# The end of layer 1 by halves of the nodes, with fewer wide operations, beside layer 2's products

## The chip, the cores and the metric

The kernel runs on one core of a Trainium2 chip. The metric is the device time of one execution in microseconds (us); smaller is better.

## The reference

Four graph layers run one after the other on 4096 nodes with 64 features, over one dense 4096 x 4096 adjacency matrix of zeros and ones. Each layer normalises x, clips it at zero to h, and adds the layer's result to x:

```
h = maximum(layernorm(x), 0)
x = x + layer(h, adj)
```

Layer 0 is graph attention with eight heads. Layer 1 works in a ball: for every pair of nodes it computes a sigmoid weight and a logarithmic map, sums them to one vector per node (`support_t`), and finishes node by node:

```
def mobius_add(x, y, c):
    x2, y2, xy = sum(x*x), sum(y*y), sum(x*y)
    num = (1 + 2*c*xy + c*y2) * x + (1 - c*x2) * y
    return num / clip(1 + 2*c*xy + c*c*x2*y2, MIN_NORM)
def expmap(p, u, c):
    u_norm = norm(u)
    return mobius_add(p, tanh(0.5*sqrt(c)*lambda_x(p, c)*u_norm) * u / (sqrt(c)*u_norm), c)
out = proj(expmap(x, support_t, c), c)      # proj: scale down where the norm is too large
```

Layer 2 averages the neighbours (`adj @ X + X` over the degree), multiplies by a matrix, and normalises each row. Layer 3 sums each row's last hundred neighbours with weights that fall by a half.

## The kernel before

Node number b*128 + p stands on partition p, in column b, so `x` and `h` are tiles of 128 partitions x 32 columns x 64 features. An operation over all of it has 128x2048 elements; `halves` names the two halves of 16 columns, 128x1024 each. A number for each node (a norm, a dot product) is a tile of 128x32, or 128x16 for a half.

**Order of the work.** A planner orders each engine's instructions by its own costs, keeping data dependences; a block under `in_order()` keeps its own order on VectorE, ScalarE and TensorE, though the planner may put other instructions between those of the block. Pools of on-chip memory are opened and closed as a stack: a tile in a new pool waits for the tiles that stood there before.

**Layer 1, pairs** (`pairs_fast`). Blocks of pairs are worked through on TensorE, ScalarE and VectorE; the sums collect in `VT` (128 x 4096), from the accumulators `acci` and `accj` (L2260, L2291, L2292, L2318). The products `pvt` (L2347, 32 in 8 groups) fold VT and turn it to nodes, and VectorE puts each group, scaled by `pabs`, into `VQ` (L2351): 64 features and one number per node. In the trace each of these fp32 products appears as two records. VT's memory belongs to the pairs' pool, and the pvt products have banks of their own.

**Layer 1, end** (`finish`). All nodes at once, on VectorE: `dot` multiplies two wide tiles and reduces (L2036, L2038), `norm_of` takes a root on ScalarE (L2043, L2044), and wide products with one number per node (`over`) follow (L2357 to L2397). Each intermediate vector is formed in full width, and its norm and dot products are then taken from it. The last step adds to x (L2397).

**Layer norm** (`layernorm_relu`, L966 to L976), for each half: mean, subtract, square on VectorE (`ln_sq`, L970), reduce (`ln_var`, L972), root on ScalarE (L973), reciprocal, multiply (L975), maximum (L976). It is called before layers 1, 2 and 3, and with another pool before layer 0.

**Layer 2** (`layers_fast`). `HH` holds h in two halves of precision; it is made in four groups of 8 columns (hs and HH, L2439 to L2442). For each half of the targets (hf) and each of 8 mask tiles `m` of 1 MB (L2448; three buffers), TensorE runs 16 products `nacc` (L2453) and 16 `dc`, which count neighbours (L2465). A tile covers four of the 32 columns, so the first four tiles of a pass read half 0 of the nodes and the last four half 1. A tail of small steps per half follows (L2473 to L2530).

**The edge test** (`count_odd`, L949 and L950). The adjacency has to be 0 or 1 throughout; 64 strips `raw` of 1 MB each are loaded and tested on VectorE, with two buffers, wherever the text places them: 12 in layer 2, 36 in layer 3. In layer 2 the text places one after the nacc products of each mask tile but every fourth:

```
if q % 4 != 3:
    count_odd(work, next(todo))
```

Layer 3 starts with loads of its weights (w3f), products psup and the steps SS and lo (L2595 to L2602).

Of the kernel before, what the change touches and what calls it, by code (L numbers as in the profile page):

```python
# [24 lines left out]
P = 128  # L25
# [805 lines left out]
def kernel(  # L831
# [124 lines left out]
    def small(name, width=NB):  # L956
        return spool.tile([P, width], F32, name=name, tag=name)

    def layernorm_relu(pool=None, tag="wide"):
        with ExitStack() as ln:  # L960
            wide = pool or ln.enter_context(tc.tile_pool(name="ln", bufs=1))
            for bs in halves:
                nb = bs.stop - bs.start
                hb = h[:, bs]
                mean = small("ln_mean", nb)
                nc.vector.tensor_reduce(mean, x[:, bs], AX.X, ALU.add)  # L966
                nc.vector.tensor_scalar(mean, mean, 1.0 / D, None, ALU.mult)
                nc.vector.tensor_tensor(hb, x[:, bs], over(mean, D), ALU.subtract)
                sq = wide.tile([P, nb, D], F32, name="ln_sq", tag=tag)
                nc.vector.tensor_tensor(sq, hb, hb, ALU.mult)  # L970
                var = small("ln_var", nb)
                nc.vector.tensor_reduce(var, sq, AX.X, ALU.add)  # L972
                nc.scalar.activation(var, var, AF.Sqrt, bias=eps_t, scale=1.0 / D)  # L973
                nc.vector.reciprocal(var, var)
                nc.vector.tensor_tensor(hb, hb, over(var, D), ALU.mult)  # L975
                nc.vector.tensor_scalar(hb, hb, 0.0, None, ALU.max)  # L976
# [1028 lines left out]
    def scalar_tile(name):  # L2005
        return lp.tile([P, 1], F32, name=name)
# [7 lines left out]
    c2, m2c, cneg, lnr, bz, be, maxn, hrow = (  # L2014
        scalar_tile(n) for n in ("c2", "m2c", "cneg", "lnr", "bz", "be", "maxn", "hrow")
    )
    nc.vector.tensor_tensor(c2, cc, cc, ALU.mult)
    nc.vector.tensor_scalar(m2c, cc, -2.0, None, ALU.mult)
    nc.vector.tensor_scalar(cneg, cc, -1.0, None, ALU.mult)
# [86 lines left out]
    def pairs_fast(es, VQ):  # L2106
# [12 lines left out]
        pabs = fp.tile([P, NB], F32, name="pabs")  # L2119
# [49 lines left out]


        VT = fp.tile([P, N], F32, name="VT")
        work = es.enter_context(tc.tile_pool(name="pfwork", bufs=2))
        with ExitStack() as ss:
# [162 lines left out]
        nc.vector.tensor_scalar(pabs, pabs, sqc, 2.0, ALU.mult, ALU.mult)  # L2336
        fold_v = work.tile([P, D1], F32, name="fold_v", bufs=1)
        nc.vector.tensor_copy(fold_v[:, 0:D], ident[:, 0:D])
        nc.vector.tensor_tensor(
            fold_v[:, D:], ident[:, D + 31 : D + 32], ident[:, P - 1 :], ALU.add  # L2340
        )
        with tc.tile_pool(name="ps_vt", bufs=2, space=PSUM) as ps:
            for g in range(NG):
                pt = ps.tile([P, GB, D1], F32, name="pvt", tag="misc")
                for b in range(GB):
                    c = (g * GB + b) * P
                    nc.tensor.matmul(  # L2347
                        pt[:, b, :], lhsT=VT[:, c : c + P], rhs=fold_v, start=True, stop=True
                    )
                bs = slice(g * GB, (g + 1) * GB)  # L2350
                nc.vector.tensor_tensor(VQ[:, bs, :], pt, over(pabs[:, bs], D1), ALU.mult)  # L2351

    def finish(VQ, wide, lp):

        V = VQ[:, :, 0:D]
        qq = dot(wide, lp, h, V, "xv")
        nc.vector.scalar_tensor_tensor(qq, qq, m2c, VQ[:, :, D], ALU.mult, ALU.add)  # L2357
        u = V
        nc.vector.tensor_tensor(u, u, over(pc, D), ALU.mult)
        t = wide.tile([P, NB, D], F32, name="hq", tag="wide")  # L2360
        nc.vector.tensor_tensor(t, h, over(qq, D), ALU.mult)
        nc.vector.tensor_tensor(u, u, t, ALU.subtract)
        rowf = small("rowf")
        nc.vector.tensor_scalar(rowf, pm, hrow, None, ALU.mult)
        nc.vector.tensor_tensor(u, u, over(rowf, D), ALU.mult)
        un = norm_of(lp, dot(wide, lp, u, u, "uu"), "un")
        nc.vector.tensor_scalar(un, un, sqc, None, ALU.mult)
        arg = small("arg")
        nc.vector.reciprocal(arg, pm)
        nc.vector.tensor_tensor(arg, arg, un, ALU.mult)  # L2370
        nc.scalar.activation(arg, arg, AF.Tanh)
        nc.vector.reciprocal(un, un)
        nc.vector.tensor_tensor(arg, arg, un, ALU.mult)
        nc.vector.tensor_tensor(u, u, over(arg, D), ALU.mult)

        y2 = dot(wide, lp, u, u, "y2")
        xy = dot(wide, lp, h, u, "xy")
        nc.vector.tensor_scalar(xy, xy, m2c, -1.0, ALU.mult, ALU.mult)
        nc.vector.tensor_scalar(xy, xy, 1.0, None, ALU.add)
        num = small("mnum")  # L2380
        nc.vector.scalar_tensor_tensor(num, y2, cc, xy, ALU.mult, ALU.add)
        den = small("mden")
        nc.vector.tensor_tensor(den, a, y2, ALU.mult)
        nc.vector.scalar_tensor_tensor(den, den, c2, xy, ALU.mult, ALU.add)
        nc.vector.tensor_scalar(den, den, MIN_NORM, None, ALU.max)
        nc.vector.reciprocal(den, den)
        nc.vector.tensor_tensor(u, u, over(pc, D), ALU.mult)
        t = wide.tile([P, NB, D], F32, name="hn", tag="wide")
        nc.vector.tensor_tensor(t, h, over(num, D), ALU.mult)
        nc.vector.tensor_tensor(u, u, t, ALU.add)  # L2390
        nc.vector.tensor_tensor(u, u, over(den, D), ALU.mult)

        nn = norm_of(lp, dot(wide, lp, u, u, "pp"), "nn")
        nc.vector.reciprocal(nn, nn)
        nc.vector.tensor_scalar(nn, nn, maxn, 1.0, ALU.mult, ALU.min)
        nc.vector.tensor_tensor(u, u, over(nn, D), ALU.mult)
        nc.vector.tensor_tensor(x, x, u, ALU.add)  # L2397

# [5 lines left out]
    def layers_fast(es):  # L2404
# [16 lines left out]
        layernorm_relu()  # L2421
        with ExitStack() as l2:
# [12 lines left out]
            OG = 8  # L2435
            for b0 in range(0, NB, OG):
                bs = slice(b0, b0 + OG)
                hs = work.tile([P, OG, D], F32, name="hs", tag="hs")
                nc.vector.tensor_scalar(hs, h[:, bs], VALH, None, ALU.mult)  # L2439
                nc.scalar.copy(HH[:, bs, 0, :], hs)  # L2440
                nc.vector.tensor_tensor(hs, hs, HH[:, bs, 0, :], ALU.subtract)
                nc.scalar.activation(HH[:, bs, 1, :], hs, AF.Copy, scale=LO)  # L2442
            for hf in range(2):
                accs = [ps_acc.tile([P, G], F32, name="nacc", tag="nacc") for _ in range(NS)]
                dc = ps_acc.tile([P, G], F32, name="dc", tag="nacc")
                for q in range(NQ):
                    m = work.tile([P, JT, HW], U8, name="m2", tag="m2", bufs=3)
                    nc.sync.dma_start(m, mask_d[q][hf])  # L2448
                    m8 = m.bitcast(F8)
                    for t in range(JT):  # L2450
                        j = q * JT + t
                        for k in range(NS):
                            nc.tensor.matmul(  # L2453
                                accs[k],
                                lhsT=HH[:, j].rearrange("p s d -> p (s d)"),
                                rhs=m8[:, t, k * G : (k + 1) * G],
                                start=(j == 0),
                                stop=(j == NB - 1),
                            )
                    if q % 4 != 3:  # L2460
                        count_odd(work, next(todo))
                    for t in range(JT):
                        j = q * JT + t
                        for k in range(NS):
                            nc.tensor.matmul(  # L2465
                                dc[k * O : (k + 1) * O, :],
                                lhsT=sel[:, j * O : (j + 1) * O],
                                rhs=m8[:, t, k * G : (k + 1) * G],
                                start=(j == 0),
                                stop=(j == NB - 1),  # L2470
                            )
# [202 lines left out]
    def after_pairs(pairs):  # L2674
        with ExitStack() as es:
            vp = es.enter_context(tc.tile_pool(name="vq", bufs=1))
            VQ = vp.tile([P, NB, D1], F32, name="VQ")
            with ExitStack() as pe:
                pairs(pe, VQ)
            wide = es.enter_context(tc.tile_pool(name="finwide", bufs=2))  # L2680
            fl = es.enter_context(tc.tile_pool(name="fin", bufs=1))
            finish(VQ, wide, fl)

    with tc.If(general == 0):
        after_pairs(pairs_fast)
        with ExitStack() as es:
            layers_fast(es)
# [61 lines left out]
```

## Time and profile before

| what | us |
|---|---|
| median of 3 runs | 2256.92 (2254.91 to 2257.21) |
| the profiled execution, its own time | 2256.87 |
| its span | 2254.9 |
| TensorE (PE) busy | 1920.0 (85%) |
| VectorE (DVE) busy | 1780.3 (79%) |
| ScalarE (ACT) busy | 1588.5 (70%) |
| last acci product of the pairs ends | 1810.9 |
| first nacc product of layer 2 starts | 1889.25 |
| layer 2's nacc and dc products end | about 1974.7 |

The profile is one execution. PE is TensorE's products, PEld its weight loads, POOL GpSimd, SP the engine that issues most transfers. A row of the timeline has start, length, engine, line and operation, tiles and shapes; "x2" means two merged. In the chain that ended last each row has start, length and what the end of the program waited for then. In the waits, "A <- B: 74.6, 1, 74.6" says that A's engine sat idle before A until B ended, in total, how often, and the longest.

### The profile page before, as it was taken

The page shows a single profiled execution, that of the slowest core. Times are in us where ns is not written, and L with a number is a line of the kernel's source. Part 1 is how long each engine was busy: PE and PEld are TensorE (multiplying, and loading weights), DVE is VectorE, ACT ScalarE, POOL GpSimd, SP SyncE. Part 2 cuts the span into 40 slices and gives each one's busy share as a digit, 9 for nine tenths or more (in the row PEclk, how much of TensorE's full clock was granted, in tenths as well). Part 3 has the DMA queues.
Part 4 walks back from the last instruction along what each step waited for, and adds up shares of the span by engine and source line. Part 5 has one row for each costly group of instructions (what it writes and reads, how often), then busy time and mean ns, then how long its engine had stood idle before and what let it go on. Part 6 is the DMA issues. An engine that isn't in the chain of part 4 may idle for free.

```text
span 2254.9 us, 43716 instructions
## 1 busy us (share of the span) xinstructions
PE 1920.0 (85%) x19276; PEld 870.7 (39%) x19276; DVE 1780.3 (79%) x2092; ACT 1588.5 (70%) x1338; POOL 86.2 (4%) x124
## 2 busy tenths in 40 slices
PE   4989989999999999769982789999999914959998
PEld 3444444444444444424441233333333401434332
DVE  6689889987898899797657899898898887463551
ACT  4678888996898799467853788888888800124765
POOL 1000101100000000001101000000000000000000
PEclk8999999999999999779996799999999966956998
DMA  9945554352111110477630001110011007624883
GB/s 112 182 100 94 91 90 114 128 192 86 44 63 67 45 52 2 145 255 252 193 109 24 18 23 33 38 33 24 28 33 38 15 0 266 257 92 176 314 313 98
DMA packets 117007, 239.00 MB, mean 106 GB/s; under 512 B 11059, under 2 KB 84003, under 8 KB 102051
## 3 DMA queue, kind: packets, MB, share of 16 engines
q1 hardware_dynamic: 101990, 192.92, 24.9%
q0 software_dynamic: 14816, 43.18, 10.8%
q8 instruction: 153, 2.51, 0.5%
q14 instruction: 48, 0.39, 0.1%
HBM read 245.34 MB, written 49.46 MB: 131 GB/s over the span
## 4 chain that ended last, share of the span: by engine, by line
PE 34%; DVE 15%; DMA 6%; ACT 4%; issue 4%; POOL 0%; SPq 0%; DVEq 0%; POOLq 0%; ACTq 0%
PE accj L2260 6%; DMA raw<-in_adj_dram 5%; PE acco L1948 5%; PE pu L2227 3%; PE nacc L2453 3%; PE pl L2196 2%; PE pf L2298 2%; PE pl L2199 2%; DVE at L2249 2%; DVE raw L950 2%; PE accC L1521 2%; DVE at L2254 1%; PE ddo L1961 1%; PE accB L1521 1%; PE tr L982 1%
## 5 line engine op out<-in xcount | busy, mean ns | idle before, releaser
L1185 ACT ACTIVATE st<-srow,nt 128x2048 int8<-128x2048 f32 x352 | 682.8, 1994 | 77.4 <-DVE B L1191 76.5
L1191 DVE TENSOR_TENSOR B<-st,mres 128x1024 int32<-128x1024 int32 x256 | 311.8, 1220 | 66.4 <-PE accC L1521 41.5
L1521 PE MATMUL accB<-B,ybh 128*32 128x512 fp8e4 x3072 | 338.1, 383 | 15.6 <-DVE B L1191 15.6
L1521 PE MATMUL accD<-B,ybh 128*32 128x512 fp8e4 x2048 | 300.5, 386 | 23.8 <-DVE h L1637 23.8
L1521 PEld LDWEIGHTS <-ybh 128*32 128x32 bf16 (+1 forms) x6656 | 196.6, 98 | 238.7 <-issue 76.4
L1521 PE MATMUL accC<-B,ycn 128*32 128x512 fp8e4 x2272 | 266.6, 379 | 1.2 <-issue 1.2
L1521 PE MATMUL accC<-mres,ych 128*32 128x512 fp8e4 x2272 | 266.6, 379 | 0.0
L1521 PE MATMUL accL<-B,ybh 128*32 128x512 fp8e4 x1536 | 219.6, 389 | 4.6 <-DVE h L1641 4.5
L950 DVE SCALAR_TENSOR_TENSOR raw<-raw 128x2048 f32<-128x2048 f32 x64 | 146.3, 2288 | 92.0 <-DMA raw<-in_adj_dram 92.0
L2260 PE MATMUL accj<-sg,VQ 128*64 128x512 f32 (+1 forms) x512 | 198.3, 615 | 18.6 <-DVE VT L2318 7.1
L1521 PEld LDWEIGHTS <-ych 128*32 128x32 f16 x4096 | 168.2, 98 | 114.0 <-issue 8.2
L1179 DVE TENSOR_SCALAR st<-srow,nt 128x2048 uint8<-128x2048 f32 x160 | 205.5, 1285 | 2.5
L2260 PE MATMUL acci<-sg,VQ 128*64 128x512 f32 (+1 forms) x512 | 197.7, 615 | 0.0
L2183 ACT ACTIVATE sg<-pl,rb 128x512 f32<-128x512 f32 x256 | 163.1, 684 | 47.3 <-PE pl L2199 43.3
L2644 ACT ACTIVATE w3b<-pv 128x1024 int16<-128x1024 f32 x128 | 131.1, 1024 | 54.6 <-PE pv L2635 54.3
L1185 ACT ACTIVATE st<-srowo,nto 128x1024 int8<-128x1024 f32 x128 | 137.3, 1137 | 42.0 <-DVE B L1191 41.8
L2227 PE MATMUL pu<-XAf,LDf 66*128 66x512 f32 x288 | 149.1, 621 | 7.2 <-DVE at L2234 5.9
L1521 PE MATMUL accC<-C,ych 128*32 128x512 fp8e4 x1824 | 145.9, 388 | 0.8 <-DVE C L1199 0.8
L1199 DVE TENSOR_TENSOR C<-B,mres 128x1024 int32<-128x1024 int32 x114 | 139.6, 1225 | 3.6
L1521 PEld LDWEIGHTS <-ycn 128*32 128x32 f16 x2272 | 107.3, 97 | 63.5 <-issue 2.4
L2453 PE MATMUL nacc<-m,HH 128*128 128x512 fp8e4 x256 | 62.0, 391 | 74.6 <-ACT HH L2442 74.6
L2234 DVE TENSOR_SCALAR at<-pu 128x512 f32<-128x512 f32 x144 | 95.2, 684 | 22.7 <-PE pu L2227 21.9
(491 smaller groups left out, 3144.2 us busy)
## 6 DMA issues: line engine op xcount, KB each, us to landing
raw<-in_adj_dram SPq DMA_DIRECT2D x64, 1024.0 KB, 7.3
mo<-edges SPq DMA_DIRECT2D x32, 512.0 KB, 4.8
noedge<-nmo POOLq DMA_DIRECT2D x32, 512.0 KB, 5.0
nm<-noedge SPq DMA_DIRECT2D x64, 256.0 KB, 3.0
m<-edges SPq DMA_DIRECT2D x16, 1024.0 KB, 6.2
m<-edges SPq DMA_DIRECT2D x32, 512.0 KB, 5.9
srow<-srow_d SPq DMA_DIRECT2D x15, 1024.0 KB, 6.5
mres<-in_adj_dram POOLq DMA_DIRECT2D x8, 1024.0 KB, 35.9
```

Source lines behind the costliest of these rows:

```text
L950: nc.vector.scalar_tensor_tensor(raw, raw, 0.0, raw, ALU.is_gt, ALU.not_equal, accum_out=bad[:, c : c + 1])
L1179: nc.vector.tensor_scalar(st[:, i, :].bitcast(U8), srow, negs[:, i : i + 1], EDGE, ALU.is_gt, ALU.mult)
L1185: nc.scalar.activation(st[:, i, :], srow, AF.Sign, bias=negs[:, i : i + 1], scale=-1.0)
L1191: nc.vector.tensor_tensor(B.bitcast(I32), st.bitcast(I32), edges.bitcast(I32), ALU.bitwise_and)
L1199: nc.vector.tensor_tensor(C.bitcast(I32), B.bitcast(I32), edges.bitcast(I32), ALU.bitwise_xor)
L1521: ins = nc.tensor.matmul(acc[k * O : (k + 1) * O, :], lhsT=values, rhs=moving(k), start=start, stop=stop,)
L1948: sums = nc.tensor.matmul(acc[k], lhsT=Y[:, i].rearrange("p s d -> p (s d)"), rhs=E[:, i, k * G : (k + 1) * G], start=j0 + i == 0, stop=ac ...
L2183: tc.keep_in_program_order(nc.scalar.activation(*args, **kw))
L2227: nc.tensor.matmul(pu, lhsT=LD[:, j * P : (j + 1) * P], rhs=XA[:, grp(gi)], start=True, stop=True,)
L2260: nc.tensor.matmul(acc[r : r + n, :], lhsT=XQ[:, src, cols], rhs=w, start=start, stop=stop)
L2453: nc.tensor.matmul(accs[k], lhsT=HH[:, j].rearrange("p s d -> p (s d)"), rhs=m8[:, t, k * G : (k + 1) * G], start=(j == 0), stop=(j == NB ...
L2644: nc.scalar.activation(w, pv, AF.Relu)
```

## The change

1. `finish` becomes `finish_steps`, a generator for one half of the nodes. The norms and dot products of the intermediate vectors are worked out from numbers by node: `xu` (h with the sum), `uu` (its square norm), `a` (h with itself). The vector itself is formed once at the end, as one factor (`arg`) times V plus another (`num`) times h. The one square that remains is on ScalarE (`vv`).
2. The pvt products and VQ's evictions move into `finish_steps`. VT, `fold_v` and `pabs` move to the pool that also holds VQ and stays open through layers 2 and 3; `fold_v` is set before the pairs.
3. Layer norm is a generator too (`norm_steps`). Its square goes to ScalarE (not before layer 0), and multiply and maximum become one VectorE instruction. `finish_steps` ends with it.
4. HH is made by halves, in the same generator (`nodes`), without the first wide multiply.
5. `side_by_side` runs half 0's steps; at each point where half 0 waits for another engine it takes two steps of half 1, ten at most. The rest of half 1 follows. All of it stands under `in_order()`.
6. In layer 2's text the edge tests stand in tiles 4 to 7 of the first pass and in all of the second, 12 as before.

```diff
+    def norm_steps(bs, wide, tag, act=True):
...
+        nc.vector.tensor_reduce(mean, x[:, bs], AX.X, ALU.add)
+        yield False
+        nc.vector.tensor_scalar(mean, mean, 1.0 / D, None, ALU.mult)
+        nc.vector.tensor_tensor(hb, x[:, bs], over(mean, D), ALU.subtract)
+        yield False
+        sq = wide.tile([P, nb, D], F32, name="ln_sq", tag=tag)
+        if act:
+            nc.scalar.activation(sq, hb, AF.Square)
+        else:
+            nc.vector.tensor_tensor(sq, hb, hb, ALU.mult)
+        yield act
+        var = small("ln_var", nb)
+        nc.vector.tensor_reduce(var, sq, AX.X, ALU.add)
+        nc.scalar.activation(var, var, AF.Sqrt, bias=eps_t, scale=1.0 / D)
+        yield True
+        nc.vector.reciprocal(var, var)
+        nc.vector.scalar_tensor_tensor(hb, hb, 0.0, over(var, D), ALU.max, ALU.mult)
+        yield False
...
+    def side_by_side(first, second, fill, most):
+        for wait in first:
+            for _ in range(min(fill, most) if wait else 0):
+                next(second)
+                most -= 1
+        for _ in second:
+            pass
...
+    nc.vector.tensor_scalar(p2c, cc, 2.0, None, ALU.mult)
...
-    def finish(VQ, wide, lp):
...
+    def finish_steps(hf, VQ, VT, fold_v, pabs, wide, ps):
...
+        for g in range(hf * NG // 2, (hf + 1) * NG // 2):
+            pt = ps.tile([P, GB, D1], F32, name="pvt", tag="misc")
...
+            nc.vector.tensor_tensor(VQ[:, gs, :], pt, over(pabs[:, gs], D1), ALU.mult)
+            yield g % 2 == 0
+        t = fat("xv")
+        nc.vector.tensor_tensor(t, hb, V, ALU.mult)
+        yield False
+        xu = scal("xu")
+        nc.vector.tensor_reduce(xu, t, AX.X, ALU.add)
+        yield False
...
+        nc.vector.tensor_tensor(t, hb, over(g, D), ALU.mult)
+        yield False
+        nc.vector.tensor_tensor(V, V, t, ALU.subtract)
+        t = fat("vv")
+        nc.scalar.activation(t, V, AF.Square)
+        yield True
...
+        nc.vector.tensor_reduce(uu, t, AX.X, ALU.add)
...
+        nc.scalar.activation(un, un, AF.Sqrt)
+        yield True
...
+        nc.scalar.activation(arg, arg, AF.Tanh)
+        yield True
...
+        nc.scalar.activation(pp, pp, AF.Sqrt)
...
+        yield True
...
+        nc.vector.tensor_tensor(V, V, over(arg, D), ALU.mult)
+        yield False
+        t = fat("xn")
+        nc.vector.tensor_tensor(t, hb, over(num, D), ALU.mult)
+        yield False
+        nc.vector.tensor_tensor(V, V, t, ALU.add)
+        yield False
+        nc.vector.tensor_tensor(x[:, bs], x[:, bs], V, ALU.add)
+        yield False
+        yield from norm_steps(bs, wide, "fat")
...
-        layernorm_relu()
...
+            def nodes(hf):
+                yield from finish_steps(hf, *sums, wide, ps)
+                bs = halves[hf]
+                hs = wide.tile([P, HB, D], F32, name="hs", tag="fat")
+                nc.scalar.activation(HH[:, bs, 0, :], h[:, bs], AF.Copy, scale=VALH)
+                yield True
+                nc.vector.scalar_tensor_tensor(
+                    hs, h[:, bs], VALH, HH[:, bs, 0, :], ALU.mult, ALU.subtract
+                )
+                nc.scalar.activation(HH[:, bs, 1, :], hs, AF.Copy, scale=LO)
+
+            with in_order():
+                side_by_side(nodes(0), nodes(1), 2, 10)
...
-                    if q % 4 != 3:
+                    if hf or q >= NQ // 2:
                         count_odd(work, next(todo))
```

## The prediction

> **What bounds the kernel now.** I read the busy time by stage first: the stretches are the end of layer 1's pairs, the end of layer 1, and layer 2's two passes. Columns are length, then busy time of PE, PEld, DVE, ACT, POOL, granted clock, DMA share, GB/s.
>
> ```profile
> 1754.00:1811.00 57.00, 54.63 (x303) 23.62 (x296) 44.91 (x42) 42.20 (x42) 0.00 (x0) 1.00 0.05 14
> 1811.00:1889.20 78.20, 2.08 (x16) 1.80 (x16) 73.39 (x67) 7.00 (x11) 3.82 (x6) 0.53 0.21 81
> 1889.20:1928.10 38.90, 38.85 (x257) 15.23 (x258) 19.02 (x21) 3.98 (x7) 0.00 (x0) 0.93 0.89 326
> 1928.10:1974.70 46.60, 46.51 (x344) 23.98 (x344) 24.37 (x48) 7.57 (x18) 2.23 (x5) 1.00 0.59 225
> ```
>
> From 1811.0 to 1889.2 VectorE alone works (73.4 of 78.2 us). Before it and after it TensorE is full. The waits of TensorE say the same, in one entry:
>
> ```profile
> PE nacc L2453 <- ACT HH L2442: 74.6, 1, 74.6
> ```
>
> The timeline gives the prices: a half-size operation, a strip of the edge test (raw), a dependent pair of small ones.
>
> ```profile
> 1881.74 1.21 DVE L975 TENSOR_TENSOR h<-h,ln_var 128x1024 f32<-128x1024 f32 x1
> 1888.46 2.28 DVE L950 SCALAR_TENSOR_TENSOR raw<-raw 128x2048 f32<-128x2048 f32 x1
> 1890.67 0.68 DVE L2441 TENSOR_TENSOR hs<-hs,HH 128x512 f32<-128x512 f32 x1
> 1850.93 0.23 DVE L2378 TENSOR_SCALAR xy<-xy,m2c 128x32 f32<-128x32 f32 x1
> 1851.20 0.18 DVE L2379 TENSOR_SCALAR xy<-xy 128x32 f32<-128x32 f32 x1
> ```
>
> A strip holds VectorE 2.21 us (1888.46 to 1890.67). Half-size operations start 1.14 us apart where independent, 1.25 where one needs the other; I take 1.20. Small ones are 0.08 to 0.27 apart; I take 0.18. The last thing to read is where pvt, the products that fold VT, lie now (chain that ended last), and how long a strip's transfer takes (tile raw, 1886 to 1896, then 2060 to 2215):
>
> ```profile
> 1781.72 1.73 PE pvt L2347 x16
> 1787.35 1.29 PE pvt L2347 x12
> DMA to landing us min/median/max: 5.1/5.1/5.1
> ...
> DMA to landing us min/median/max: 5.6/7.3/8.1
> ```
>
> So most pvt products stand in the full TensorE stage today, and a strip lands in 5.1 us when it has the queues nearly to itself, 7.3 when it shares them with layer 3's masks.
>
> [...]here layer 2's first 16 products take 6.11 us against 3.56 later, and that stays.[...] a load is 1.28 us here, and the changed order holds six small activations with five loads, behind which VectorE has other work.
>
> **Part 1, the end of layer 1.** Let T0 be the end of the last pairs product (acci, 1810.93 now). Today it takes 4.2 us to the first wide operation, 54.3 for `finish` (21 full-width operations), 16.6 for the norm and 3.2 for HH: 78.3 us to the first nacc product. In the built program I counted what stands on VectorE between T0 and the first half's HH:
> - three moves into VT, 0.69+0.71+0.72 = 2.1 us;
> - all eight VQ evictions, since pvt now waits for the last VT sum and for the banks of the pairs: TensorE makes a group in 0.55 us (8 in 1.11 us for two), so 8×0.55+0.5 = 4.9;
> - 19 half-size operations, 14 of half 0 and 5 of half 1, ×1.20 = 22.8;
> - 53 small ones ×0.18 = 9.5;
> - **all 12 strips of layer 2**. In the text of the kernel they stand behind the products, but the built order pulls them in between the steps of half 0. 12×2.22 = 26.6;
> - what ScalarE leaves open: the norm's root 0.45, the HH copy 1.2, its low part 1.3 (128x1024 on ScalarE takes 1.14 in layer 0): 2.95. The squares, tanh and the other roots have a strip or other steps beside them.
>
> The sum is 68.9. Today one strip lies there, and a second starts as the stage ends. The strips' transfers start at T0, three masks first: 5 MB at the 420 GB/s of 1870 to 1882 is 12.5 us, and VectorE reaches the first strip at about T0+14.5. After that a strip is asked for when the one two before it is done, 5.4 to 7.5 us before its turn. At 5.1 us nothing waits; at 7.3 a pair of strips takes 9.5 us instead of about 8.2, up to 6.5 us in all. I take 1.5. First nacc at T0+70.4: **−7.9 us**, between −9.5 and −2.
>
> **Part 2, half 1 beside the products.** Behind half 0 VectorE has 9 half-size operations (11), 27 small (4.9) and open ScalarE steps (4.2): HH of half 1 at about T0+89.2. TensorE needs it after four mask tiles: 70.4 + 7.1 (cold) + 3×4.53 = T0+91.1. Hidden, by under 2 us; late by up to 3 in the range. The fourth mask waits for the first tile's release and has 9 us to land: enough. Layer 2's passes stay 38.9 + 46.6, since TensorE is full in both now; taking the strips out of them gains nothing.
>
> **Part 3, T0 itself.** The pvt pieces before T0 add up to 4.3 us on the chain (the two above, and 0.37, 0.17, 0.39, 0.17, 0.17). TensorE is 96% busy there, so their going should show; VectorE and ScalarE (79% and 74%) can take some back. −1.5 to −4.3, I take **−3**. Three small reductions (qsel, bsel, fold_h) move into VectorE's idle time before T0: free, 0.9 us if not.
>
> **Part 4, the norms of the other layers.** Before layer 1 (1178 to 1192) VectorE loses a square (1.1 net, to ScalarE, idle then) and two maxima (0.6 and 0.7); half 1's square goes to ScalarE and comes back no sooner. By the steps the dot product a_w starts at 1189.4 instead of 1191.69, and no longer stands behind rabs, which waits for the load of r. The load is issued after the last variance, so it moves too. −2.3, less 0.3 for fold_v after the branch: **−2.0**, from −1 to −3. In the first norm, before layer 0, two maxima go: **−0.5** (0 to −1.2). Before layer 3 a ScalarE square now stands in front of the last group's square: the steps give x complete at 2007.8, as now. One strip more comes ahead of the first `lo`: **+0.5** (−1 to +1.5). p2c and the added small steps elsewhere: nothing, under 0.2.
>
> **Sum.** −7.9−3−2.0−0.5+0.5 = −12.9 us. The profiled execution is 2256.87 us (span 2254.9), its median of three 2256.92: **2244.0**.
>
> **Rivals.**
> - *The strips set the pace* (slower). If each strip comes late, half 0 stands behind all 12. My order gives one per 4.1 us. Layer 3's 36 strips run at 5.7 us each (2008.6 to 2212), with masks between them; at that pace 11 intervals add 17.6 us: 2262. It decides from 5.3 us on (12.9/11 more). Against it: no mask is in the queue between strips here, and alone they land in 5.1. At 4.9, layer 3's pace between 2150.7 and 2199.7, it is 2253.
> - *Half 1 is late.* TensorE idles before the fifth tile; each us late is a us: 8 us late gives 2252. For it: the small margin. Against it: the chain behind half 0 meets no strip.
> - *The change doesn't do what it says*: if the strips hold back half 0 so long that only half 1's tail runs beside products, the gain is parts 3 and 4 alone, 5 us: 2252.
> - *More*: T0 −4.3, no waits at the strips, small operations mostly at 0.1: 2236.
>
> **How the numbers follow.** About 0.2%, 4.5 us, is what can be told from no change here: the border is 2252.4. As forecast, 2236 to 2250: 0.71. More than that: 0.07. Half 1 late, or only the tail hidden, 2250 to 2257: 0.17, a little over half of it under the border. Strips at layer 3's pace: 0.05. Faster 0.88, same 0.07, slower 0.05. The range 2235 to 2255 takes in the bounds of parts 1 to 4 and most of the third case.
>
> **What would show it.** Right: nacc waits once, about 64 us instead of 74.6 (pvt now ends later, at T0+6.6), with 12 strips ahead of it and waits of raw for its transfer under 5 us in all; no wait of nacc at the fifth tile; pvt in one block of about 4.5 us after T0; layer 2's passes still 39 and 47 us. Wrong: raw waiting more than 13 us before the first nacc, or nacc waiting for HH twice. If T0 to the first nacc is under 66 us, my small operations were too dear.

## The result, and the profile after

The changed kernel takes 2244.77 us (median of 7 runs, 2234.51 to 2246.54), the kernel before 2256.92 in the same comparison (7 runs, 2253.19 to 2259.78): ratio 0.9934, 95% interval 0.9913 to 0.9954. The forecast was 2244.0. The number is right; the way to it, as the profile shows, is not. The profiled execution took 2246.54 us with a span of 2244.6.

Busy time by stage, kernel after (length, then busy time of PE, PEld, DVE, ACT, POOL, granted clock, DMA share, GB/s): the end of the pairs, the end of layer 1, layer 2's two passes, the start of layer 3, the rest of layer 3.

```profile
1753.20:1813.20 60.00, 53.26 (x262) 18.37 (x263) 47.62 (x45) 44.77 (x43) 2.30 (x4) 1.00 0.06 14
1813.20:1890.80 77.60, 13.69 (x65) 13.54 (x66) 63.53 (x114) 13.08 (x16) 0.74 (x2) 0.52 0.57 203
1890.80:1927.40 36.60, 36.60 (x239) 14.55 (x240) 14.39 (x31) 3.92 (x6) 0.00 (x0) 0.95 0.54 191
1927.40:1976.50 49.10, 48.95 (x362) 24.49 (x360) 18.07 (x42) 8.42 (x20) 2.22 (x5) 1.00 0.38 137
2009.00:2061.00 52.00, 35.75 (x168) 18.74 (x172) 30.21 (x46) 23.01 (x39) 2.68 (x3) 0.69 0.64 225
2061.00:2244.60 183.60, 166.54 (x748) 56.68 (x760) 75.09 (x80) 121.36 (x121) 6.42 (x9) 0.93 0.68 241
```

The same view of the kernel before, for layer 3 alone:

```profile
2008.00:2060.00 52.00, 39.97 (x129) 20.16 (x130) 25.95 (x40) 16.34 (x28) 2.59 (x3) 0.50 0.46 163
2060.00:2254.90 194.90, 180.41 (x805) 60.95 (x804) 80.44 (x86) 127.21 (x130) 6.45 (x9) 0.91 0.70 243
```

The second line of after is the stage that the change was about: 77.6 us where 78.2 stood. VectorE's 73.4 busy us fell to 63.5, but TensorE has 13.7 there where it had 2.1. The passes add up to 85.7, 85.5 before. The last pair of lines holds the gain: in the first 52 us of layer 3 TensorE had a mean clock of 0.69 instead of 0.50 and left 168 records of products instead of 129 in less busy time. Taking starts of instructions throughout, the 10.3 us between the two spans split so:

| piece | before | after | difference |
|---|---|---|---|
| start to last acci product | 1810.3 | 1812.4 | +2.1 |
| last acci to first nacc (end of layer 1) | 78.9 | 78.4 | -0.5 |
| first to last nacc | 84.1 | 84.3 | +0.2 |
| last nacc to first psup | 56.4 | 56.3 | -0.1 |
| first to last psup | 36.9 | 24.7 | **-12.2** |
| last psup to end | 188.3 | 188.5 | +0.2 |

Tile psup, before and then after (durations minimum/median/maximum in ns, first and last start):

```profile
L2595 PE MATMUL psup<-w3f,hT x64: 417/418/473, 2029.7 to 2066.6; 64*128 64x64 f32 x64
```

```profile
L2659 PE MATMUL psup<-w3f,hT x64: 272/272/472, 2031.4 to 2056.1; 64*128 64x64 f32 x64
```

The code of these products was not touched. At least half of them run at 272 ns after, and none under 417 before. The granted clock is 0.50 under all of before's (2029.7 to 2066.6); in after it is 0.50 until 2040.9 and 1.00 from there on. These two readings are called half and full clock below.

The views that the prediction named. TensorE's wait for HH, after:

```profile
PE nacc L2517 <- ACT HH L2502: 61.8, 1, 61.8
```

The strips between the pairs and layer 2 (tile raw, after, 1800 to 1890; the two lines in the middle are what VectorE waited for):

```profile
L950 DVE SCALAR_TENSOR_TENSOR raw<-raw x12: 2280/2282/2292, 1837.4 to 1881.9; 128x2048 f32<-128x2048 f32 x12
...
its engine sat idle before it (us, times) until:
  DMA raw<-in_adj_dram: 0.2, 1
...
DMA to landing us min/median/max: 5.0/5.1/14.1
```

One wait of nacc, so half 1 was in time (its HH is ready at 1909.6, the fifth tile's products start at 1910.55); twelve strips in the stage, as the built order said, and 0.2 us lost to their transfers. And the pvt block, timeline of after (start, length, engine; in brackets the idle time before it and what ended it):

```profile
1815.35 13.67 PE L2376 MATMUL pvt<-fold_v,VT 128*128 128x65 f32 x64 [2.33 <-DVE VT L2338]
1817.11 0.43 DVE L2380 TENSOR_TENSOR VQ<-pvt,pabs 128x260 f32<-128x260 f32 x1 [1.91 <-PE pvt L2376]
1818.81 0.43 DVE L2380 TENSOR_TENSOR VQ<-pvt,pabs 128x260 f32<-128x260 f32 x1 [1.28 <-PE pvt L2376]
...
1829.52 1.22 DVE L2383 TENSOR_TENSOR xv<-h,VQ 128x1024 f32<-128x1024 f32 x1
```

An eviction every 1.71 us, each waiting for TensorE: 13.7 us where 4.9 were forecast. The count of the first line says why: 64 records for 32 products, so eight records are one group and not two.

### The profile page after: what moved, and what is told of

The parts are those of the page before. It is cut to its first block, busy times and chain, and to the rows that moved or that the text cites. A ratio compares the mean times of both kernels' runs of the same rounds, so it can differ in the third digit from the quotient of the medians.

```text
span 2244.6 us, 43714 instructions
## 1 busy us (share of the span) xinstructions
PE 1912.7 (85%) x19229; PEld 872.8 (39%) x19276; DVE 1749.8 (78%) x2128; ACT 1599.9 (71%) x1347; POOL 84.6 (4%) x124
## 4 chain that ended last, share of the span: by engine, by line
PE 35%; DVE 16%; ACT 5%; DMA 5%; issue 4%; POOL 0%; SPq 0%; DVEq 0%; POOLq 0%; ACTq 0%
PE accj L2280 6%; PE acco L1971 4%; DMA raw<-in_adj_dram 4%; PE pu L2247 3%; PE nacc L2517 3%; DVE raw L950 3%; PE pf L2318 2%; PE pl L2216 2%; DVE at L2269 2%; PE pl L2219 2%; PE accC L1544 2%; ACT sg L2203 1%; DVE at L2274 1%; PE accB L1544 1%; PE ddo L1984 1%
## 5 line engine op out<-in xcount | busy, mean ns | idle before, releaser
L1208 ACT ACTIVATE st<-srow,nt 128x2048 int8<-128x2048 f32 x352 | 682.8, 1994 | 78.3 <-DVE B L1214 77.5
L2517 PE MATMUL nacc<-m,HH 128*128 128x512 fp8e4 x256 | 60.8, 387 | 61.8 <-ACT HH L2502 61.8
```

Source lines behind the costliest of these rows:

```text
L1208: nc.scalar.activation(st[:, i, :], srow, AF.Sign, bias=negs[:, i : i + 1], scale=-1.0)
L2517: nc.tensor.matmul(accs[k], lhsT=HH[:, j].rearrange("p s d -> p (s d)"), rhs=m8[:, t, k * G : (k + 1) * G], start=(j == 0), stop=(j == NB ...
```

## Experiments

Two questions: what the stage at the end of layer 1 is made of, and why layer 3 became shorter. All kernels compute everything. Each ratio is to runs of the kernel before in the same comparison (medians 2257.85, 2255.24 and 2255.71 in the three groups), with its 95% interval. "Half clock" is the stretch from layer 2's last products into layer 3, in windows of 3.413 us: this is the shortest stretch at one clock in the clock records of before and after, and every other stretch there is a whole number of it (up to 59), but for the last, which the end of the program cuts. So the changes of the clock lie on a grid with that period.

| kernel | us | ratio | last acci to first nacc | psup first to last | half clock |
|---|---|---|---|---|---|
| before | 2256.92 | | 78.9 | 36.9 | 27 |
| after | 2244.77 | 0.9934 | 78.4 | 24.7 | 18 |
| e1 norms alone | 2232.52 | 0.9891 | 75.0 | 20.4 | 14 |
| e2 strips behind | 2222.88 | 0.9841 | 55.2 | 25.3 | 18 |
| e3 pvt in the tail | 2227.46 | 0.9875 | 63.8 | 25.0 | 18 |
| e4 both | 2208.46 | 0.9788 | 41.5 | 25.2 | 18 |
| e5 old norm 3 | 2236.74 | 0.9917 | 78.3 | 24.5 | 18 |
| e6 before, warm | 2239.57 | 0.9928 | 78.9 | 19.3 | 13 |
| e7 both, warm | 2204.66 | 0.9774 | 41.5 | 21.0 | 13 |
| e8 after again | 2244.21 (one run) | | 78.6 | 24.9 | 18 |
| e9 before, 1.4 later | 2247.41 | 0.9974 | 78.9 | 26.5 | 19 |
| e10 before, 2.3 later | 2245.62 | 0.9962 | 78.9 | 24.4 | 18 |
| e11 before, 3.45 later | 2258.38 | 1.0019 | 78.9 | 36.9 | 28 |
| e12 before, 5.75 later | 2246.98 | 0.9970 | 78.9 | 24.3 | 19 |

**e1, the norms alone.**

```diff
 (kernel before, all else unchanged)
-    def layernorm_relu(...): square on VectorE, product, maximum
+    def norm_steps(...), layernorm_relu(...) of the changed kernel
```

> The kernel before with the norms alone as after the change (square on ScalarE, maximum and product in one step, in all three places where the norm is called); the end of layer 1 stays as before. If the norms are worth only their own steps (part 4 of the prediction: -2.0 before layer 1, -0.5 before layer 0, and now also the norm before layer 2, which lies in VectorE's 78 us stage: two squares and two maxima less, about -3.5), the time is about 2251, and layer 3 starts with its psup groups at 1.97 us (half clock) for some 40 us as before. Rival: the changed norm before layer 3 (third strip ahead of the first lo) is what lets TensorE reach full clock at 2041 instead of 2060 to 2070 in the profile after; then layer 3's last part shortens by about 11 us as well, and the time is about 2240.

2232.52 us, 0.9891 [0.9871, 0.9910]: more than the whole change brings. The end of layer 1, with the new norm in it but the old `finish`, is 75.0 us, 3.9 shorter than before (expected 3.5). The rest is layer 3:

```profile
L2608 PE MATMUL psup<-w3f,hT x64: 271/272/321, 2028.7 to 2049.1; 64*128 64x64 f32 x64
```

All groups ran at full clock (1.00 in every 4 us from 2028 to 2052), 20.4 us from first to last. So layer 3's gain needs nothing of the new end of layer 1. Whether it needs the new norm is the question of e5.

**e2, strips behind.**

```diff
+            behind = last VectorE instruction of side_by_side(...)
...
-                        count_odd(work, next(todo))
+                        count_odd(work, next(todo), behind)   # an order on VectorE, no wait
```

> The changed kernel with one order added: layer 2's 12 strips of the edge test may stand on VectorE only behind half 1's last step, so none lies between the pairs and the first nacc product. By the prediction's price (12 x 2.22 us) the stretch from the last pairs product to the first nacc goes from 77.6 to about 51 us, and layer 2's two passes stay at 85.5 us, because TensorE is full in them: time about 2245 - 26 = 2219. Rival 1: pass one stalls, because half 1 is still 19 us behind half 0, and because the third strip's transfer, which waits for the first strip's test behind half 1, stands in front of a mask in SP's queue: 5 to 10 us come back, 2224 to 2229. Rival 2: the strips filled time in which VectorE would have waited anyway (roots, squares, tanh on ScalarE): then less than 15 us is gained, 2230 or more.

0.9841 [0.9811, 0.9872]; the six runs lie between 2209 and 2228 us. TensorE's wait for HH:

```profile
PE nacc L2527 <- ACT HH L2510: 38.6, 1, 38.6
```

It is 61.8 in after: the strips cost 23.2 us of the 26.6 that their VectorE time is, so, by this sum, 3.4 of it had filled waits. First to last nacc is 85.8 instead of 84.3, and still nacc waits for HH only once. Rival 1 holds for 1.5 us, rival 2 falls.

**e3, pvt in the pairs' tail.**

```diff
     (end of pairs_fast, in banks of its own, as before)
+        for g in range(NG): pvt products, VQ[:, gs, :] = pt * pabs
     (finish_steps)
-        for g in range(hf * NG // 2, (hf + 1) * NG // 2): pvt products, VQ
-                side_by_side(nodes(0), nodes(1), 2, 10)
+                side_by_side(nodes(0), nodes(1), 2, 6)
```

> The changed kernel with the pvt products and their eight evictions back where they stood before (in banks of their own behind the pairs' products, most of them ahead of the last pair). The profile after shows the pvt block at 13.7 us after the last VT sum. If it stands on the path with all of that, the stretch to the first nacc loses 13.7 less about 1.5 for the last groups, and the pairs' tail takes back up to 4.3 us: about 2236. Rival: the first strips' transfers, which start at the same time and land about 14 us later, take the place of the pvt block: then raw waits 8 to 10 us and the time is about 2243.

0.9875 [0.9852, 0.9898]. The stage is 14.6 us shorter than in after, a little more than the 12.2 expected, and the pairs' tail takes nothing back: from the norm's a_w to the last acci it is 620.4 us here and 620.4 in after.

**e4, both edits together.** The diffs of e2 and e3.

> Both edits: pvt back in the pairs' tail, and layer 2's strips behind half 1. If the two gains are independent, the stretch from the last pairs product to the first nacc is about 40 us and the time 2245 - 26 - 9 = 2210. Rival: masks now bound the start: the first three masks land about 14 us after the pairs, which is earlier than that, so it should not; half 1, 19 us behind half 0, could be late for the fifth tile (20.6 us after the first product): each us late is a us.

0.9788 [0.9766, 0.9811], 2208.46 us. The stage is 41.5: 36.9 less than after, where e2 and e3 save 23.2 and 14.6. The two gains add up to within 1 us.

**e5, the old norm before layer 3, the rest changed.**

```diff
-        layernorm_relu()          # before layer 3
+        layernorm_first()         # the function of the kernel before
```

> The changed kernel with one part undone: the norm before layer 3 is as before (square on VectorE, maximum as a step of its own); all else as changed. Theory A: that norm decides what stands on VectorE between it and layer 3's first products[...]: then TensorE stays at half clock through all psup groups again, first to last psup 35 to 37 us instead of 24.7, and the time is about 2245 + 11 = 2256. Theory B: the early full clock comes from elsewhere (chance, or when layer 3 starts): psup stays at 20 to 25 us and the time is 2245 to 2247.

Theory A is wrong: psup 24.5 us, time 2236.74, 0.9917 [0.9898, 0.9936], an interval that overlaps that of after, so the 8 us between the medians are not read as an effect. Yet in layer 3 the order of VectorE, TensorE and SyncE here is, instruction for instruction, that of the kernel before. psup groups in the timeline of before, and then of e5:

```profile
2033.49 1.97 PE L2595 MATMUL psup<-w3f,hT 64*128 64x64 f32 x8
2038.09 1.97 PE L2595 MATMUL psup<-w3f,hT 64*128 64x64 f32 x8
2045.26 1.97 PE L2595 MATMUL psup<-w3f,hT 64*128 64x64 f32 x8
```

```profile
2031.92 1.97 PE L2678 MATMUL psup<-w3f,hT 64*128 64x64 f32 x8
2036.52 1.53 PE L2678 MATMUL psup<-w3f,hT 64*128 64x64 f32 x8
2040.89 1.10 PE L2678 MATMUL psup<-w3f,hT 64*128 64x64 f32 x8
```

The same groups, 4.6 us apart in both, and in e5 the clock rises within the second of these. Same order, other clock: what differs is where the products lie on the clock's grid. Plate is a pair of products just ahead of layer 3's others. Of the two, after, e8 and e5 kept only the second in the trace, but both weight loads; in after:

```profile
2020.43 0.14 PEld L2635 LDWEIGHTS <-lat 128*128 128x128 bf16 x2 [16.90 <-issue]
2020.84 0.63 PE L2635 MATMUL plate<-cnt,lat 128*128 128x512 bf16 x1 [17.12 <-DVE lat L2623]
```

So positions are given here by plate's first weight load. From the rise of the clock in layer 2 to it, it is 124.4 us in before, 124.1 in e1, and 126.3, 126.4 and 126.8 in after, e8 and e5.

**e6, sixteen added products.**

```diff
                 nc.tensor.matmul(pl, lhsT=lat, rhs=cnt16[:, hf], start=True, stop=True)
+                for _ in range(16 if hf else 0):
+                    nc.tensor.matmul(pl, lhsT=lat, rhs=cnt16[:, hf], start=True, stop=True)
```

> The kernel before with 16 added products 128x512 bf16 (the second plate product sixteen times more, same result) between plate and layer 3's first pv products; nothing else changed. They take 3 to 7 us and put off pv and psup by 3 to 5 us. If half clock under the psup groups is what makes layer 3 long in the kernel before, TensorE is at full clock when pv begins, first to last psup takes about 20 us instead of 37, and the time falls by 17 - 4 = 13 us to about 2244. Rival: psup's pace comes from its evictions or from the strips on VectorE: then psup stays above 30 us and the time is 2256 to 2262.

0.9928 [0.9904, 0.9951], 2239.57 us: the kernel before with work added is as fast as the changed one. Busy time of e6 at the start of layer 3, where the clock rises inside the first line:

```profile
2023.00:2028.00 5.00, 5.00 (x21) 2.15 (x20) 4.61 (x7) 0.23 (x2) 0.00 (x0) 0.76 0.44 136
2028.00:2033.00 5.00, 5.00 (x35) 3.09 (x33) 3.25 (x7) 4.26 (x7) 0.00 (x0) 1.00 0.72 280
```

psup takes 19.3 us. The rival falls: the half clock goes and psup's length with it. But the run is less clean than its edit: with the added products the planner also put layer 3's strips, masks and evictions in another order on VectorE, ScalarE and SyncE. That the clock sets psup's pace is seen without this in e5, where groups in the old order go from 1.97 to 1.10 us as it rises.

**e7, e4 with the sixteen products.** The diffs of e4 and e6; the planner changed layer 3's order here too.

> The version with pvt in the pairs' tail and the strips behind half 1 (2208.5 us), with the same 16 added products behind plate. First to last psup was 25.2 us there and the clock rose about 15 us after layer 3's first products: with the added products at the front psup should take about 20 us and start 3 to 5 us later: 2206 to 2209, a gain of 2 us at most. If the clock's rise differs between executions of that version, the spread should become smaller.

2204.66 us, 0.9774 [0.9756, 0.9791]; its interval overlaps that of e4. The runs lie within 1.6 us, those of e4 within 5.5. It is the fastest version run.

**e8, the changed kernel once more.**

> The changed kernel once more, unaltered, for a second profile. If the instant at which layer 3 reaches full clock depends on where the 3.41 us windows fall and so differs between executions, psup may take 20 us or 37 instead of 24.7, with the time moving by as much; if the order of instructions alone sets it, psup takes 24 to 25 us again. The stretch from the last pairs product to the first nacc should be 78 us again in either case.

2244.21 us, psup 24.9, end of layer 1 78.6: as in the first profile. Layer 3's shorter start is no accident of one execution.

**e9 to e12, the kernel before with a delay ahead of layer 3.** n is 3, 5, 7, 12; the last two have one more step of 128x64. The order on TensorE, VectorE, ScalarE and SyncE in layer 3 is that of before.

```diff
                     nc.vector.tensor_tensor(zt, zt, over(nrm, D), ALU.mult)
+                    for _ in range(n if hf and g == NS - 1 else 0):
+                        nc.vector.tensor_tensor(zt, zt, zt, ALU.max)
```

> The kernel before with 3 useless VectorE steps (maximum of zt with itself, 128x256, about 0.46 us each, same values) in the last group of layer 2, on the chain to layer 3: everything from there on 1.4 us later, the order on every engine otherwise as before. Theory A (the clock's grid): the distance from the clock's rise in layer 2 to plate was 124.4 us in the kernel before and 126.7 to 127.2 in three executions that had full clock 9 windows of 3.41 us sooner in layer 3. This one lies between, 125.8, so either may come: 2246 or 2257. Theory B (more work, more time): 2255.2 + 1.4 = 2256.6.

> The same with 5 useless steps, 2.3 us. Theory A: distance 126.7 us, as in the changed kernel, so TensorE gets full clock after 18 windows instead of 27, psup takes 24 to 25 us instead of 37, and the time falls by 12 - 2.3 = 10 us to about 2245, although work was added and nothing taken away. Theory B: 2257.5.

> The same with 7 useless steps and one of 128x64, 3.45 us, one whole period of the grid. Theory A: the products of layer 3 lie on the grid as in the kernel before, so half clock lasts 27 windows and a period more, psup takes 37 us, and the time is 2255.2 + 3.4 = 2258.7. Theory B gives the same here; a fall to 2246 to 2250 would speak against a grid of 3.41 us and for a mere delay that helps (for instance because a strip or a mask has landed by then).

> The same with 12 useless steps and one of 128x64, 5.75 us, which is 2.3 us plus one period. Theory A: as with 5 steps on the grid: psup 24 to 25 us, time 2255.2 + 5.75 - 12 = 2249. Theory B: 2261.

Ratios: 0.9974 [0.9953, 0.9994], 0.9962 [0.9940, 0.9985], 1.0019 [1.0007, 1.0032], 0.9970 [0.9957, 0.9984]. Tile psup of e10, e11 and e12:

```profile
L2599 PE MATMUL psup<-w3f,hT x64: 272/272/473, 2035.2 to 2059.6; 64*128 64x64 f32 x64
```

```profile
L2599 PE MATMUL psup<-w3f,hT x64: 417/418/473, 2036.5 to 2073.4; 64*128 64x64 f32 x64
```

```profile
L2599 PE MATMUL psup<-w3f,hT x64: 272/272/472, 2035.1 to 2059.4; 64*128 64x64 f32 x64
```

Useless work of 2.3 us makes the kernel 8.6 us faster (0.0038 of 2255.7), work of one period makes it slower by about itself, and 2.3 us plus a period makes it fast again. A grid of that period explains all three; a strip or a mask that lands late enough would have helped at 3.45 us too. The distances from clock rise to plate agree: 126.6, 127.8 and 130.1 us; the last two less one period are 124.4 and 126.7. e9, at 125.7, gave times from 2237 to 2267, and its profiled execution a psup of 26.5: it lies between, as it was expected to. (In the expectation of e9 the 126.7 to 127.2 of three executions run to the second plate product; to the first they are 0.4 less.)

## Why the prediction was right in its number and wrong in its steps

**What bounds the kernel, and the clock.** That the stage belongs to VectorE held: in e2, where strips leave VectorE, it shrinks by 23 us. That layer 2's first products stay slow held in part: the first 16 take 6.11 us in before and 5.25 in after, with the clock at 0.50 until 1894.3 and 1894.1; later 16 take 3.63, at 1.00.

The clock falls 4.86 to 4.93 us after the end of the last acci product in all ten traces with pvt in the pairs' tail, and 2.56 to 2.59 us after it in the four without. Windows of 3.413 us without a tie to the program would spread these over 3.4 us; 0.07 and 0.03 us were measured. What ties them is open; but so a position on the grid can belong to a kernel and come again in its next execution.

In layer 2 the rise to 1.00 comes between 3.1 and 6.0 us after the first product. In layer 3 of the kernel before it came at 2072, after TensorE had read busy throughout for 47 us such as these:

```profile
2028.00:2033.00 5.00, 5.00 (x20) 2.86 (x18) 0.85 (x2) 1.46 (x3) 0.00 (x0) 0.50 0.91 338
2048.00:2053.00 5.00, 5.00 (x20) 2.98 (x18) 1.03 (x3) 1.56 (x4) 0.00 (x0) 0.50 0.00 0
```

The prediction priced the start of layer 3 by the order of its steps alone, +0.5, with no term for the clock there. This is the step that failed by most: 12.2 us less was measured.

**Part 1 failed, by 7 us.** Forecast 78.3 to 70.4, measured a gain of 0.5. The failed term is pvt and VQ, 4.9 us. "8 in 1.11 us for two" groups took records for products, although two records for each had been noted. The line of before that gives the price:

```profile
1813.50 1.10 PE L2347 MATMUL pvt<-fold_v,VT 128*128 128x65 f32 x8 [1.53 <-DVE VT L2318]
```

These 8 records are 4 products, one group, at full clock (1.00 until 1815.8). At that price eight groups are 8.9 us; in after the block also runs at half clock (0.50 from 1816.2 to 1829.1), 1.71 for each group, 13.7 us. The other terms were right in their sum: from the first xv (1829.52) to the first nacc it is 61.3 us, against 70.4 - 2.1 - 4.9 = 63.4. Of the difference, 1.3 is the wait for strips (1.5 forecast, 0.2 measured). The 12 strips were priced at 26.6 and cost 23.2 (e2). xv takes 1.22 us in after (128x1024), xv_w in before 2.29 (128x2048): here halving the nodes did not quite halve the price. The five loads that the prediction counts are ScalarE's table loads (ACT_TABLE_LOAD, 1.28 us each), and five stand in the stage of after.

**Part 2 held.** Half 1 hidden by 1 us (under 2 forecast), nacc waiting once, passes 85.7 for 85.5.

**Part 3 failed.** Forecast -3; from a_w to the last acci it is 618.6 in before and 620.4 and 618.4 in the two profiles of after, and with pvt back there 620.4 (e3) and 620.1 (e4). Over all 14 traces it is 618.4 to 620.4 without pvt in the tail and 618.6 to 621.5 with it: no gain that stands out of the scatter. The 4.3 us on the chain of waits were TensorE's, but when they went TensorE stood idle instead: 53.3 busy in the last 60 us, where it had 54.6 in 57. A share of the chain was taken for a saving.

**Part 4** held before layer 1: last evB copy to a_w is 23.8 us before, 22.2 and 21.7 after; in all traces 23.3 to 24.7 with the old norm there and 19.3 to 22.4 with the new. The first norm's 0.5 cannot be seen: that copy lies between 1167.0 and 1173.6 in the executions here. Before layer 3 the forecast was +0.5 and the psup stretch lost 12.2: right in "one strip more comes ahead of the first lo", blind to the clock.

**The sum.** -7.9 - 3 - 2.0 - 0.5 + 0.5 was to be -12.9. It became about -0.5, nothing, -1.6, nothing seen and -12.2, with 3.7 us more ahead of the last acci (1.9 before the last evB copy, 1.8 in the pairs; single executions scatter by more, the last acci starting between 1809.0 and 1816.4). That the total agrees is chance.

**The rivals.** Strips at a slower pace: excluded, 0.2 us of waits. Half 1 late: excluded. *The change doesn't do what it says* came nearest in its effect, though by another way: the end of layer 1 gains nearly nothing, and with layer 3 as before the time would be 2244.77 + 12.2 = 2257, that of the kernel before.

**Cause of layer 3's gain.** Shown: it is the clock (groups of the same form take 1.97 us in before, at 0.50, and 1.10 in e5 after the rise), and with layer 3's order unchanged the position on the grid decides it (e5, e10 to e12). The change moves that position: the first nacc product comes 5.1 us ahead of the clock's rise in before and 3.3 in after, and from nacc to plate it is 0.2 us more; together 2.0 us, near the 2.3 of e10. The change also gives layer 3 a new order, through the norm, and that order has full clock at every position seen: 124.1 us (e1, 14 windows) and 125.1 to 126.4 (e2, e4, after, e8, e3; 18 windows). The old order has it only at the later ones. So in the changed kernel either would be enough by itself, and their parts are not separated; e1 stands 0.2 us from before, and the old order was not run just there. Open: what makes the clock rise. That psup groups hold it down is not the whole answer: the kernel before had a window without one, with TensorE busy throughout (2024.0 to 2027.4), and the clock stayed at 0.50 after it.

## What to carry to other kernels

Count records per product before pricing a product from a trace: pvt's 32 fp32 products left 64. Look where a planner puts work that the text places later; here twelve strips and one block cost 37 us in a place where the next stage waits for them, and an order and an earlier place (e4) returned them. Where a stage of TensorE starts after idle time, read its clock over tens of us (here 0.50 for 92 us), and shift the stage by 1 to 3 us before believing that an edit elsewhere sped it up or slowed it down.

## What was not expected of the hardware

TensorE stayed at half clock (0.50, from 1979.6 to 2071.8 in before) for 27 windows, 92 us, of which it read busy for the last 47, in a mix of 64-column fp32 groups with wide bf16 and fp8 products. Added work shortened the time: sixteen products by 0.7%, three, five and twelve VectorE steps by 0.3 to 0.4%. The rest of layer 3, from last psup to end, has the same order in before and e9 to e12, and took 174.9 to 188.3 us. It goes with the time at half clock in that stretch: 27.9, 19.4, 13.3, 11.6 and 6.0 us at half clock where it took 188.3, 183.3, 181.2, 180.6 and 174.9 (before, e11, e9, e10, e12). No run tests which of the two makes the other. In the third group, 4 of 61 runs of the kernel before lie under 2243 us; the good position may also come by itself, seldom, but these runs left no trace.
